# A four-layer graph network on one core: layer 1's order and buffers, and a dense first block in layer 2

## The chip, the core and the metric

The kernel runs on one core of one Trainium2 chip. The core has a matrix engine (PE, with its weight loads shown apart as PEld), a vector engine (DVE), a scalar engine (ACT), a general engine (POOL) that here mostly issues gathers, and a queue engine (SP) that issues plain transfers. Sixteen DMA engines move the data. The metric is the time of one execution in device microseconds; less is better. All data is float32.

## What is computed

There are 2708 nodes with 512 features each, and a 2708 x 2708 adjacency matrix in which about 0.15% of the entries and the diagonal are not zero (uniform between 0.05 and 1). Four layers follow each other, each with a residual sum and a layer norm:

```python
x = layernorm(x + L0(x, adj))
x = layernorm(x + L1(x, adj))
x = layernorm(x + L2(x, adj))
x = layernorm(x + L3(x, adj))

# L0:  (x - (adj @ x) * (diag + 1)) @ W + b
# L1:  h = x @ W_sa;  e = where(adj != 0, exp(-leaky_relu(s_left[:, None] + s_right[None, :])), 0)
#      x_a = (e / (e.sum(1) + 1e-5)) @ h;  x_b = adj @ (x @ W_gc) + b_gc
#      sigmoid(gate_a * x_a + gate_b * x_b)     # the gates from adj @ x and x
# L2:  head = (adj > 0); head = head / max(sqrt(sum(head * head, -1)), 1e-12)
#      inc = adj + head;  (inc @ x) / inc.sum(-1)
# L3:  A = adj + I; d = A.sum(0) ** -0.5;  tanh((d * A * d) @ x @ W.T + b)
```

In layer 2 the row norm of `head` depends on the row alone, so an entry of `inc` is the value of the edge plus one number of its row wherever the value is positive.

## The kernel before

Rows are cut into 24 blocks (`NB`) of 113 nodes (`R`); the last has 109. There are 22 windows (`KB`) of 128 nodes as well, for the dense projections of layer 0. Nothing is planned at run time: each engine executes its instructions in the order in which the code writes them, and waits where another engine's or a transfer's result is needed.

In layer 0 (to some 413 us of the span) the columns of the adjacency for a block are loaded (`load_adj`, L673 and L677), the edges are found on DVE, and each block gets a list of at most 512 source nodes (four chunks, `EC`), with values in `edges`. The rows of x are gathered, and each block writes a row of 1029 numbers (`W1`) per node into a table in DRAM, `table[0]`. All layers after that work from the lists: POOL gathers the 512 source rows of a block with four indirect transfers (`gather`, L600), and PE multiplies them by a 512 x 113 selection matrix that DVE builds from the list.

**Layer 1** (some 411 to 615 us). For each block, POOL gathers four times 128 x 1029 from `table[0]`, and for the blocks from 6 on also the block's own rows (`gather_own1`, L1382) into one of `NO` = 6 places in buffers that are no longer used; the first six own blocks come by plain loads at the end of layer 0 (`load_own1`). PE forms two sums: `sums1` (l1s, L1427) and `scored_sums1` (l1e, L1437). DVE works through `both1` (L1472 to L1483), `scores1` (L1410, L1414), `stats1` (L1492 to L1508, with a power on POOL in L1509), `gates1`, `gated1` (L1457, L1461, which read l1s), `mask1` (L1420), and `source_sum`. `norm1` (ACT, L1524) writes the normed rows into SBUF (`xr`) and SP stores them to `table[1]`. The l1s sum has one buffer in PSUM. At the end of layer 1 the column sums of the adjacency go through DRAM (`deg_d`, `deg_r`, L1556 and L1558), and the bias and weight of layer 3 (`b3`, `w3`) are loaded by SP.

**Layer 2** (some 615 to 768 us). Each block gathers four times 128 x 512 from `table[1]`. DVE rebuilds the selection matrix (`values`, L1294) and adds the norm of the row (`incidence`, L1612 and L1615; the norms come from `row_norms`, turned across by `turn_norm` on PE and copied by `copy_norm`). `aggregate` on PE makes l2a, `stats2` and `norm2` finish a block and store it to `table[2]`. `keep_warm` puts matmuls on PE that no one reads (`unread`, L1571). Layer 3 gathers from `table[2]`, sums, projects, and writes the output.

Every transfer of a block's 113 rows goes through `move_rows`, which issues two:

```python
c = r // 16 * 16
for a, b in ((0, c), (c, r)):
    if a < b:
        nc.sync.dma_start(out=dst(a, b), in_=src(a, b))
```

The end of layer 1 reads, in the order of the code: `both1(23)`, `stats1(23)`, `scale1`, `norm1(23)`, then `values(0)`, `incidence(0)`, `values(1)`, `incidence(1)`, then the gathers of layer 2's blocks 0 and 1, and the loop over 24 blocks.

Of the kernel before, what the change touches and what calls it, by code (L numbers as in the profile page):

```python
# [8 lines left out]
FP = mybir.dt.float32  # L9
AF = mybir.ActivationFunctionType  # L10
ALU = mybir.AluOpType
# [436 lines left out]
def sparse_stack(  # L448
# [115 lines left out]
    def move_rows(r, dst, src):  # L564

        c = r // 16 * 16
        for a, b in ((0, c), (c, r)):
            if a < b:
                nc.sync.dma_start(out=dst(a, b), in_=src(a, b))

    def turned(u, r, name):

        tr = ps_tr.tile([P, DB, P], FP, tag="tr", name=f"tr_{name}")
        for f in range(DB):
            nc.tensor.transpose(tr[:, f, :r], u[:r, f * P : (f + 1) * P], ident[:r, :r])
        uT = work.tile([P, DB, P], FP, tag="uT", name=f"uT_{name}")
        nc.scalar.copy(uT[:, :, :r], tr[:, :, :r])  # L577
        return uT

# [46 lines left out]

    w0_own = big.tile([P, 2 * W1], FP, name="w0_sb")
    w0_sb = w0_own[:, : DB * D].rearrange("p (b d) -> p b d", d=D)
    NO = 6

    def own_place(i):
        return (*shared, w0_own)[i % NO // 2][:, i % 2 * W1 :][:, :W1]

    def load_own1(i):
        r = rows(i)
# [12 lines left out]
    with ExitStack() as phase:  # L648
# [40 lines left out]

        def load_own(i):  # L690
            r = rows(i)
            xi = work.tile([P, D], FP, tag="xi", name=f"xi{i}")
            move_rows(r, lambda a, b: xi[a:b, :], lambda a, b: x[i * R + a : i * R + b, :])
            return xi

# [122 lines left out]
        def turn_w(k):  # L818
            ps = ps_tr.tile([P, DB, P], FP, tag="tr", name=f"w_sa_t{k}")
            for f in range(DB):  # L820
                nc.tensor.transpose(ps[:, f, :], w_sa_sb[:, f, k * P : (k + 1) * P], ident)
            wT = work.tile([P, DB, P], FP, tag="uT", name=f"w_saT{k}")
            nc.scalar.copy(wT, ps)
            w_saT[k] = wT

# [225 lines left out]
        def store0(w):  # L1051
            r = wrows(w)
            st, o = st0.pop(w)
            nc.scalar.copy(st[:r, D + 1 : 2 * D + 1], o[:r, :])
            move_rows(
                r, lambda a, b: table[0][w * P + a : w * P + b, :], lambda a, b: st[a:b, :]
            )
# [3 lines left out]
        def turn_u(i):  # L1061

            u, r = u0.pop(i), rows(i)
            tr = ps_tr.tile([P, DB, P], FP, tag="tr", name=f"tr_l0_{i}")
            for f in range(DB):
                nc.tensor.transpose(tr[:, f, :r], u[:r, f * P : (f + 1) * P], ident[:r, :r])
            a = i * R
            while a < i * R + r:
                w = a // P
                b = min(i * R + r, (w + 1) * P)  # L1070
                if w not in window_uT:
                    window_uT[w] = work.tile(
                        [P, DB, P], FP, tag="uw", name=f"uw{w}", bufs=3
                    )
                nc.scalar.copy(
                    window_uT[w][:, :, a - w * P : b - w * P], tr[:, :, a - i * R : b - i * R]
                )
                a = b
# [130 lines left out]
        for k in range(NB + 2):  # L1209
            m = k + 2  # L1210
            w, wx, rest = window_at.get(k), window_at.get(k - 1), window_at.get(k - 1)
            bare = 2 < k < NB and w is None
            after = 2 < k < NB and wx is None
            parts = 4
            if any(t not in window_at for t in (k + 1, k + 2, k + 3)) and 2 < k < NB - 4:
                parts = 5
            if bare:
                parts, rest = 2, None
            if after:
                parts, rest = 3, window_at[k - 2]  # L1220
            if wx is not None and k <= NB:
                turn_x(wx)
            if m < NB:
                ranges(m)
                mark(m)
                fetch(m)
            if w is not None:
                project0(w)
            if k == 1:
                times_a(2)  # L1230
                times_a(3)
            if k == 0:
                times_a(0)
                turn_w(2)
            if unstored:
                store0(unstored.pop())
            if k + 3 < NB:
                negatives(k + 3)
            search(1)
            if m < NB:  # L1240
                pick(m)
                own[m] = load_own(m)
                values0(m)
            if k == 1:
                score_rows()
            if w is not None:
                bias0(w)
            search(1)
            if w is not None:
                residual0(w)  # L1250
            if window_at.get(k + 1, 0) > 1:
                load_window(window_at[k + 1])
            search(parts - 2)
            if wx is not None and not bare:
                next0(wx)
            if w is not None:
                norm0(w)
            if k + 1 < NB:
                sums0(k + 1)
                inputs0(k + 1)  # L1260
            if k == 1:
                score_columns()
            if k + 2 == NB:
                worst = check_lists()
                for i in range(4):
                    load_own1(i)
            if k == 0:
                times_a(1)
                turn_w(3)
            if bare:  # L1270
                starts(m + 1)
                next0(wx)
            elif rest is not None:
                rest0(rest, lambda: turn_x(w) if k == NB else starts(m + 1) if m + 1 < NB else None)
                unstored.append(rest)
            elif m + 1 < NB:
                starts(m + 1)
            if k + 1 < NB:
                turn_u(k + 1)
            if k == NB:  # L1280
                tell(worst)
                for i in range(4, NO):
                    load_own1(i)
        keep_busy(4)
        store0(KB - 1)


    gpool = ctx.enter_context(tc.tile_pool(name="gpool", bufs=1))
# [65 lines left out]
    nc.vector.memset(root, -0.5)  # L1354
    edge_s, edge_e, sum_s, sum_e, vb1, gate1, v1, mv2, unscaled = ({} for _ in range(9))
    phase = ctx.enter_context(ExitStack())
    ps_1s = phase.enter_context(tc.tile_pool(name="ps_1s", bufs=1, space=bass.MemoryType.PSUM))
    ps_1e = phase.enter_context(tc.tile_pool(name="ps_1e", bufs=1, space=bass.MemoryType.PSUM))
    ps_sp = phase.enter_context(tc.tile_pool(name="ps_sp", bufs=2, space=bass.MemoryType.PSUM))

# [230 lines left out]
            nc.scalar.sqrt(inv_norm[:, at], inv_norm[:, at])  # L1591
            nc.vector.reciprocal(inv_norm[:, at], inv_norm[:, at])

    row_in, inc2 = {}, {}

    def turn_norm(i):

# [10 lines left out]
    def incidence(i, s):  # L1608
# [5 lines left out]
        )  # L1614
        nc.vector.tensor_add(inc, inc, s)  # L1615

    b3_bc = gpool.tile([P, D], FP, name="b3_bc")
    w3_sb = shared[0][:, : DB * D].rearrange("p (b d) -> p b d", d=D)

# [9 lines left out]
    for i in range(NB):  # L1629
# [5 lines left out]
        if i + 2 < NB:  # L1635
            values1(i + 2, (0, 1))
        scored_sums1(i)
        if i + 1 == NB:
            turn_norm(0)
            turn_norm(1)  # L1640
        if i + 1 < NB:
            scores1(i + 1)
        if 0 < i < NB - 1:
            stats1(i - 1)
        if 0 < i and i - 1 + NO < NB:
            gather_own1(i - 1 + NO)
        gates1(i)
        if i + 2 < NB:
            values1(i + 2, (2, 3))
# [12 lines left out]
            nc.sync.dma_start(out=w3_sb, in_=w3T.rearrange("(b p) o -> p b o", p=P))  # L1662
        if i < KB:
            source_sum(i)
        if i == KB:
            source_sums_out()
            row_norms(slice(0, KB))
    copy_norm(0)
    copy_norm(1)
    keep_warm(ps_sp, "sp", [P, 4, P], 8)  # L1670
    both1(NB - 1)
    spread_row(b3_bc, "b3")
    stats1(NB - 1)
    scale1()
    norm1(NB - 1)
    deg_ps = source_sums_in()
    inc_s = [values(0)]
    incidence(0, inc_s[0])
    inc_s.append(values(1))
    incidence(1, inc_s[1])  # L1680
    nc.vector.tensor_copy(b3_bc, spread_ps["b3"])

    nc.vector.tensor_copy(deg[:R, :], deg_ps[:R, 0, :NB])
# [5 lines left out]
    nc.vector.tensor_add(d_inv, deg, zero)  # L1689
    nc.scalar.sqrt(d_inv, d_inv)  # L1690
    row_norms(slice(KB, NB), False)
    phase.close()
    ps_agg = ctx.enter_context(tc.tile_pool(name="ps_agg2", bufs=2, space=bass.MemoryType.PSUM))
    ps_tr = ctx.enter_context(tc.tile_pool(name="ps_tr2", bufs=1, space=bass.MemoryType.PSUM))
    ps_o = ctx.enter_context(tc.tile_pool(name="ps_o2", bufs=2, space=bass.MemoryType.PSUM))
    ps_sp = ctx.enter_context(tc.tile_pool(name="ps_sp2", bufs=2, space=bass.MemoryType.PSUM))
    ps_u = ctx.enter_context(tc.tile_pool(name="ps_u", bufs=1, space=bass.MemoryType.PSUM))


    for i in range(2):  # L1700
        gather(gath[i], i, table[1], D)
    nc.vector.tensor_add(rowsum, rowsum, adiag)
    nc.vector.tensor_mul(plus, plus, inv_norm)
# [11 lines left out]
    dself = const.tile([P, NB], FP, name="dself")  # L1715
    nc.vector.scalar_tensor_tensor(dself, adiag, 1.0, d_inv, op0=ALU.add, op1=ALU.mult)

    sum2, v2, edge_3 = {}, {}, {}

    def own2(i):  # L1720
        r = rows(i)
        v = work.tile([P, D], FP, tag="v", name=f"l2v{i}")
        nc.scalar.activation(v[:r, :], xr[:r, i, :], AF.Copy, scale=plus[:r, i : i + 1])
        v2[i] = v

    def stats2(i):
# [32 lines left out]
        move_rows(r, lambda a, b: table[2][i * R + a : i * R + b, :], lambda a, b: y[a:b, :])  # L1759

    own2(0)
    for i in range(NB):
        if i + 2 < NB:
            gather(gath[(i + 2) % NGB], i + 2, table[1], D)
            turn_norm(i + 2)
# [1 line left out]
        sum2[i] = aggregate(inc2.pop(i), gath[i % NGB], rows(i), f"l2a{i}")  # L1767
        if i + 1 < NB:
            keep_warm(ps_u, "u", [P, D], 1)
        if i > 0:  # L1770
            stats2(i - 1)
        s = values((i + 2) % NB)
        if i > 0:
            norm2(i - 1)
        if i + 1 < NB:
            own2(i + 1)
        if i + 2 < NB:
# [133 lines left out]
```

## Time and profile before

| what | value |
| --- | --- |
| median of 14 runs | 978.04 us (972.11 to 983.77) |
| the profiled execution | 976.4 us, its span 974.7 us |
| granted TensorE clock, mean | 0.968 |
| busy share of the span | PE 91%, DVE 70%, ACT 54%, POOL 48% |
| first l1s matmul of block 1 and of block 23 | 429.9 and 604.8 us |
| first layer-2 gather on POOL | 623.73 us |
| indirect gathers by list: from the tables, from x | 288 and 96 |

The page of the profile has the busy time of each engine, a strip of the span in 40 slices, the DMA queues, the chain of waits that ended last, and the costliest groups of instructions. A group's row names the line of the code, the engine, the operation, what it writes and reads, how often, its busy time in us and the mean of one in ns, and the idle time of the engine just before it with what ended it. The waits view sums, by waiting instruction and releaser, how long an engine stood. The timeline lists single instructions with start and length in us. Besides these the trace has a record of every DMA packet, with its size and the time it took, and one of every rise of a DMA's semaphore.

### The profile page before, as it was taken

To read this page: it belongs to the slowest core of one execution; us is meant where nothing else is said; L and a number is where in the kernel's file an instruction comes from. 1 tells how busy PE (TensorE), PEld (TensorE's weight loads), DVE (VectorE), ACT (ScalarE), POOL (GpSimd) and SP (SyncE) were. 2 spreads that over 40 slices of the span, in tenths; PEclk is the share of its full clock that TensorE was granted. 3 is DMA by queue.
4 is the path that set the end of the run, shared out by engine and by line. 5 is a ranking of instruction groups with operands and counts; after the bars stand their busy time and mean duration, and the time that the engine had idled before them with its cause. 6 is when DMAs were issued, how large, how long until landed. Compare 5 with 4: busy or idle time off the path is not lost.

```text
span 974.7 us, 11098 instructions
## 1 busy us (share of the span) xinstructions
PE 883.5 (91%) x2957; PEld 488.9 (50%) x2957; DVE 686.7 (70%) x1811; ACT 527.2 (54%) x1221; POOL 471.1 (48%) x521
## 2 busy tenths in 40 slices
PE   6789999999999999989989899786979889999993
PEld 2445656555555555457767677332323333444441
DVE  7797899888998833268988888766768326555553
ACT  5686767767768743457777776343535212222221
POOL 3332323313233310167777673477777476676730
PEclk7799999999999999999999999897999999999997
DMA  9988786988886534388989994466767465555531
GB/s 246 313 206 226 212 228 202 262 221 227 221 234 202 168 110 144 106 302 301 331 315 326 324 319 162 131 196 190 208 203 213 119 174 157 152 167 170 151 106 33
DMA packets 133759, 201.74 MB, mean 207 GB/s; under 512 B 82700, under 2 KB 82746, under 8 KB 133689
## 3 DMA queue, kind: packets, MB, share of 16 engines
q0 software_dynamic: 39456, 120.08, 39.9%
q1 hardware_dynamic: 94233, 80.86, 29.1%
q8 instruction: 26, 0.43, 0.2%
q14 instruction: 44, 0.36, 0.1%
HBM read 183.00 MB, written 27.80 MB: 216 GB/s over the span
## 4 chain that ended last, share of the span: by engine, by line
PE 58%; DVE 12%; issue 11%; DMA 9%; POOL 4%; ACT 2%; SPq 2%; another core or an unknown queue 1%; DVEq 0%; POOLq 0%; ACTq 0%
PE o_l L584 14%; PE l3a L613 9%; PE l2a L613 7%; DMA gath<-table,source 6%; PE h L584 6%; PE l0a L613 6%; PE hb L584 5%; POOL gath L600 3%; PE unread L1571 3%; PE fetched L915 2%; SPq L677 1%; PE l1s L1427 1%; DMA gath<-in_x_dram 1%; DVE where_all L862 1%
## 5 line engine op out<-in xcount | busy, mean ns | idle before, releaser
L600 POOL DMA_INDIRECT gath<-table,source x288 | 309.5, 1075 | 108.0 <-issue 81.9
L600 POOL DMA_INDIRECT gath<-in_x_dram,source x96 | 97.5, 1016 | 222.4 <-issue 191.0
L1427 PE MATMUL l1s<-gath,s 128*113 128x256 f32 (+3 forms) x384 | 90.2, 387 | 19.4 <-DVE l1b L1457 14.4
L613 PE MATMUL l2a<-gath,s_left 128*113 128x512 f32 (+1 forms) x192 | 95.7, 631 | 8.8 <-DMA gath<-table,source 6.7
L613 PE MATMUL l3a<-gath,s 128*113 128x512 f32 (+1 forms) x192 | 89.9, 612 | 2.8 <-DMA gath<-table,source 2.8
L584 PE MATMUL o_l<-shared,uT_l 128*113 128x512 f32 (+1 forms) x192 | 86.5, 593 | 2.6 <-ACT uT_l L577 2.6
L1437 PE MATMUL l1e<-gath,e 128*113 128x257 f32 (+3 forms) x384 | 87.1, 379 | 0.9 <-issue 0.9
L1427 PEld LDWEIGHTS l1s<-gath,s 128*113 128x113 f32 (+1 forms) x384 | 65.9, 177 | 43.8 <-DVE l1b L1457 19.8
L613 PE MATMUL l0a<-gath,s 128*113 128x512 f32 (+1 forms) x192 | 87.7, 599 | 0.0
L584 PE MATMUL hb<-w_gc_sb,uT_x 128*128 128x512 f32 (+1 forms) x176 | 83.3, 601 | 0.0
L584 PE MATMUL h<-w_sa_sb,uT_x 128*128 128x259 f32 (+1 forms) x352 | 80.8, 382 | 0.0
L584 PE MATMUL o_l<-w_sb,uw 128*128 128x512 f32 (+1 forms) x176 | 80.3, 599 | 0.2
L1437 PEld LDWEIGHTS l1e<-gath,e 128*113 128x113 f32 (+1 forms) x384 | 68.0, 177 | 16.4 <-issue 1.3
L584 PEld LDWEIGHTS h<-w_sa_sb,uT_x 128*128 128x128 f32 (+1 forms) x352 | 64.8, 185 | 19.8 <-issue 6.1
L613 PEld LDWEIGHTS l2a<-gath,s_left 128*113 128x113 f32 (+1 forms) x192 | 32.3, 185 | 62.4 <-issue 33.2
L1830 ACT ACTIVATE y<-l3v,mv_l 113x512 f32<-113x512 f32 (+1 forms) x24 | 19.6, 816 | 80.7 <-DVE mv_l L1826 74.9
L584 PEld LDWEIGHTS o_l<-shared,uT_l 128*113 128x113 f32 (+1 forms) x192 | 33.9, 178 | 51.0 <-issue 47.3
L1804 DVE SCALAR_TENSOR_TENSOR l3v<-o_l,d_inv,b_bc 113x512 f32<-113x512 f32 (+1 forms) x25 | 18.1, 729 | 57.6 <-PE o_l L584 50.3
L1571 PE MATMUL unread<-bg_bc,ident 128*128 128x512 f32 x80 | 41.7, 636 | 16.6 <-remote 13.3
L613 PEld LDWEIGHTS l3a<-gath,s 128*113 128x113 f32 (+1 forms) x192 | 33.2, 184 | 42.3 <-issue 39.3
L613 PEld LDWEIGHTS l0a<-gath,s 128*113 128x113 f32 (+1 forms) x192 | 34.0, 180 | 40.3 <-issue 35.8
L1294 DVE TENSOR_SCALAR s<-niota_r,nrow,edges 128x113 f32<-128x113 f32 x192 | 51.9, 347 | 0.0
(250 smaller groups left out, 1591.7 us busy)
## 6 DMA issues: line engine op xcount, KB each, us to landing
shared<-in_adj_dram SPq DMA_DIRECT2D x14, 1186.5 KB
table<-st SPq DMA_DIRECT2D x21, 514.5 KB
gath<-in_adj_dram SPq DMA_DIRECT2D x7, 1186.5 KB
gath<-in_x_dram SPq DMA_DIRECT2D x21, 256.0 KB
xi<-in_x_dram SPq DMA_DIRECT2D x23, 224.0 KB
table<-xr SPq DMA_DIRECT2D x23, 224.0 KB
table<-y SPq DMA_DIRECT2D x23, 224.0 KB
out_dram<-y SPq DMA_DIRECT2D x23, 224.0 KB
```

Source lines behind the costliest of these rows:

```text
L584: nc.tensor.matmul(o, lhsT=uT[:, f, :r], rhs=w[:, f, :], start=(f == 0), stop=(f == DB - 1))
L600: nc.gpsimd.indirect_dma_start(out=g[:, c, :n], out_offset=None, in_=src[:, :], in_offset=bass.IndirectOffsetOnAxis(ap=source[:, i, c : c ...
L613: nc.tensor.matmul(agg[:r, :], lhsT=s[:, c, :r], rhs=g[:, c, off : off + D], start=(c == 0), stop=(c == EC - 1),)
L677: nc.sync.dma_start(out=a[:TAIL, NF, :r], in_=adjT[NF * P :, at])
L862: nc.vector.max_index(out=where_all[:, i, g * 8 : (g + 1) * 8], in_max=top, in_values=seg)
L915: nc.tensor.matmul(t["fetched"][:, c, : 3 * NS], lhsT=t["q"][:, c * P : (c + 1) * P], rhs=rec_all[:, i].rearrange("p k s -> p (k s)"), sta ...
L1294: nc.vector.tensor_scalar(s[:, c, :], niota_r, nrow[:, i, c : c + 1], edges[:, i, c, 1:2], op0=ALU.is_equal, op1=ALU.mult,)
L1427: nc.tensor.matmul(sum_s[i][:r, k, : at.stop - at.start], lhsT=s[:, c, :r], rhs=g[:, c, at], start=(c == 0), stop=(c == EC - 1),)
L1437: nc.tensor.matmul(sum_e[i][:r, k, k : k + at.stop - at.start], lhsT=e[:, c, :r], rhs=g[:, c, at], start=(c == 0), stop=(c == EC - 1),)
L1571: nc.tensor.matmul(o[:, :cols], lhsT=ident, rhs=bg_bc[:, :cols], start=True, stop=True)
L1804: nc.vector.scalar_tensor_tensor(v[:r, at], o[:r, at], d_inv[:r, i : i + 1], b3_bc[:r, at], op0=ALU.mult, op1=ALU.add,)
L1830: nc.scalar.activation(y[:r, :], v[:r, :], AF.Identity, bias=mv[:r, 3:4], scale=mv[:r, 2:3])
```

## The change

It has three parts.

1. The buffers `xi`, `uT` and `uw` of layer 0, which came from a pool, become slots of two larger tiles, `xi_own` and `uw_own`, with as many slots each as the pool gave them. The two tiles hold three more places for own rows in layer 1 (`NO` 9 in place of 6): `load_own1(6)` is issued with 4 and 5, 7 and 8 at the end of layer 0, and 15 own gathers are left in layer 1 of 18.
2. In layer 1, l1s gets two buffers in PSUM in place of one, and `gather_own1` moves ahead of `stats1`.
3. In layer 2, block 0 is not gathered. `load_all` loads the whole columns of block 0 of the adjacency, 2708 rows of 113 numbers, into the two tiles, at the end of the iteration `i == KB`; `incidence_all` adds the norm on DVE (two instructions for four node blocks), and `sums_all` multiplies them on PE with `xr` in SBUF, 24 matmuls. The parts are spread over the end of layer 1 as the diff shows; 8 warm-up matmuls leave there. The norms of block 0 are made earlier, and the gathers begin with blocks 1 and 2.

```diff
-    NO = 6
+    uw_own = big.tile([P, 3 * D], FP, name="uw_own")
+    xi_own = big.tile([P, max(4 * D, 2 * W1)], FP, name="xi_own")
...
+    NO = 9
...
             if k == NB:
                 tell(worst)
-                for i in range(4, NO):
+                for i in range(4, 7):
                     load_own1(i)
         keep_busy(4)
         store0(KB - 1)
+        for i in range(7, NO):
+            load_own1(i)
...
-    ps_1s = phase.enter_context(tc.tile_pool(name="ps_1s", bufs=1, space=bass.MemoryType.PSUM))
+    ps_1s = phase.enter_context(tc.tile_pool(name="ps_1s", bufs=2, space=bass.MemoryType.PSUM))
...
+    NX = xi_own.shape[1] // R
+    all_in = [
+        t[:, : n * R].rearrange("p (b i) -> p b i", i=R)
+        for t, n in ((xi_own, NX), (uw_own, NB - NX))
+    ]
+    def load_all():
+        for t, a, b in ((all_in[0], 0, NX), (all_in[1], NX, NB - 1)):
+            nc.sync.dma_start(
+                out=t[:R, : b - a, :],
+                in_=adjT[a * R : b * R, :R].rearrange("(b p) i -> p b i", p=R),
+            )
+        b = NB - 1
+        nc.sync.dma_start(out=all_in[1][: rows(b), b - NX, :], in_=adjT[b * R :, :R])
+    def incidence_all(blocks):
+        for b in blocks:
...
+            nc.vector.scalar_tensor_tensor(
+                inc[:R, :n, :], t[:R, at, :], 0.0,
+                row_in[0][:R, None, :].to_broadcast([R, n, R]), op0=ALU.is_gt, op1=ALU.mult,
+            )
+            nc.vector.tensor_add(t[:R, at, :], t[:R, at, :], inc[:R, :n, :])
+    def sums_all(blocks):
...
+        for b in blocks:
+            nc.tensor.matmul(
+                sum2[0][:R, :], lhsT=all_in[b >= NX][: rows(b), b - NX * (b >= NX), :],
+                rhs=xr[: rows(b), b, :], start=(b == 0), stop=(b + 1 == NB),
+            )
...
         if i + 1 < NB:
             scores1(i + 1)
+        if 0 < i and i - 1 + NO < NB:
+            gather_own1(i - 1 + NO)
         if 0 < i < NB - 1:
             stats1(i - 1)
-        if 0 < i and i - 1 + NO < NB:
-            gather_own1(i - 1 + NO)
...
+        if i == NB - 4:
+            row_norms(slice(0, 1))
         if i == KB:
             source_sums_out()
-            row_norms(slice(0, KB))
-    copy_norm(0)
+            row_norms(slice(1, KB))
+            load_all()
+        if i + 1 == NB:
+            incidence_all((0, EC))
     copy_norm(1)
-    keep_warm(ps_sp, "sp", [P, 4, P], 8)
+    copy_norm(2)
+    sums_all(range(2 * EC))
     both1(NB - 1)
-    spread_row(b3_bc, "b3")
     stats1(NB - 1)
+    incidence_all((2 * EC,))
     scale1()
     norm1(NB - 1)
+    sums_all(range(2 * EC, 3 * EC))
+    incidence_all((3 * EC,))
+    incidence_all((4 * EC, NX))
+    incidence_all(range(NX + EC, NB, EC))
+    sums_all(range(3 * EC, NX))
+    spread_row(b3_bc, "b3")
     deg_ps = source_sums_in()
-    inc_s = [values(0)]
-    incidence(0, inc_s[0])
-    inc_s.append(values(1))
-    incidence(1, inc_s[1])
+    sums_all(range(NX, NB))
+    inc_s = [values(1)]
+    incidence(1, inc_s[0])
+    inc_s.append(values(2))
+    incidence(2, inc_s[1])
...
-    for i in range(2):
+    for i in range(1, 3):
         gather(gath[i], i, table[1], D)
...
     own2(0)
-    for i in range(NB):
+    stats2(0)
+    own2(1)
+    phase.close()
...
+    for i in range(1, NB):
```

More of the change, by code (lines that the diff above doesn't have):

```diff
@@ L569, in move_rows, with next_uT @@
                 nc.sync.dma_start(out=dst(a, b), in_=src(a, b))
+    def next_uT():
+        uT_ring.append(uT_ring.pop(0))
+        return uT_ring[-1]
     def turned(u, r, name):
@@ L575, in turned @@
             nc.tensor.transpose(tr[:, f, :r], u[:r, f * P : (f + 1) * P], ident[:r, :r])
-        uT = work.tile([P, DB, P], FP, tag="uT", name=f"uT_{name}")
+        uT = next_uT()
         nc.scalar.copy(uT[:, :, :r], tr[:, :, :r])
@@ L628, in sparse_stack @@
     w0_sb = w0_own[:, : DB * D].rearrange("p (b d) -> p b d", d=D)
-    NO = 6
+    uw_own = big.tile([P, 3 * D], FP, name="uw_own")
+    uw_ring = [uw_own[:, k * D : (k + 1) * D].rearrange("p (b i) -> p b i", i=P) for k in range(3)]
+    xi_own = big.tile([P, max(4 * D, 2 * W1)], FP, name="xi_own")
+    xi_ring = [xi_own[:, k * D : (k + 1) * D] for k in range(2)]
+    uT_ring = [
+        xi_own[:, k * D : (k + 1) * D].rearrange("p (b i) -> p b i", i=P) for k in range(2, 4)
+    ]
+    NO = 9
     def own_place(i):
-        return (*shared, w0_own)[i % NO // 2][:, i % 2 * W1 :][:, :W1]
+        k = i % NO
+        t = (*shared, w0_own, uw_own, xi_own)[(k + (k >= 7)) // 2]
+        return t[:, (k + (k >= 7)) % 2 * W1 :][:, :W1]
     def load_own1(i):
@@ L691, in load_own @@
             r = rows(i)
-            xi = work.tile([P, D], FP, tag="xi", name=f"xi{i}")
+            xi = xi_ring[i % 2]
             move_rows(r, lambda a, b: xi[a:b, :], lambda a, b: x[i * R + a : i * R + b, :])
@@ L821, in turn_w @@
                 nc.tensor.transpose(ps[:, f, :], w_sa_sb[:, f, k * P : (k + 1) * P], ident)
-            wT = work.tile([P, DB, P], FP, tag="uT", name=f"w_saT{k}")
+            wT = next_uT()
             nc.scalar.copy(wT, ps)
@@ L1071, in turn_u @@
                 if w not in window_uT:
-                    window_uT[w] = work.tile(
-                        [P, DB, P], FP, tag="uw", name=f"uw{w}", bufs=3
-                    )
+                    window_uT[w] = uw_ring[w % 3]
                 nc.scalar.copy(
@@ L1592, in row_norms @@
             nc.vector.reciprocal(inv_norm[:, at], inv_norm[:, at])
-    row_in, inc2 = {}, {}
+    row_in, inc2, sum2 = {}, {}, {}
     def turn_norm(i):
@@ L1615, in incidence @@
         nc.vector.tensor_add(inc, inc, s)
+    NX = xi_own.shape[1] // R
+    all_in = [
+        t[:, : n * R].rearrange("p (b i) -> p b i", i=R)
+        for t, n in ((xi_own, NX), (uw_own, NB - NX))
+    ]
+    def load_all():
[8 more added lines that the diff above has]
+        for b in blocks:
+            t = all_in[b >= NX]
+            b = b - NX * (b >= NX)
+            at = slice(b, min(b + EC, t.shape[1]))
+            n = at.stop - at.start
+            inc = spool.tile([P, EC, R], FP, tag="e", name=f"all{b}")
+            nc.vector.scalar_tensor_tensor(
[4 more added lines that the diff above has]
+    def sums_all(blocks):
+        if 0 in blocks:
+            sum2[0] = ps_1s.tile([P, 2, D], FP, tag="s1", name="l2all")[:, 0, :]
+        for b in blocks:
[3 more added lines that the diff above has]
+            )
     b3_bc = gpool.tile([P, D], FP, name="b3_bc")
@@ L1637, in sparse_stack @@
         scored_sums1(i)
+        if i == NB - 3:
+            turn_norm(0)
+            copy_norm(0)
         if i + 1 == NB:
-            turn_norm(0)
             turn_norm(1)
+            turn_norm(2)
         if i + 1 < NB:
             scores1(i + 1)
+        if 0 < i and i - 1 + NO < NB:
+            gather_own1(i - 1 + NO)
         if 0 < i < NB - 1:
             stats1(i - 1)
-        if 0 < i and i - 1 + NO < NB:
-            gather_own1(i - 1 + NO)
         gates1(i)
@@ L1691, in sparse_stack @@
     row_norms(slice(KB, NB), False)
[L1692 to L1697, printed above, removed]
-    for i in range(2):
+    for i in range(1, 3):
         gather(gath[i], i, table[1], D)
@@ L1716, in sparse_stack @@
     nc.vector.scalar_tensor_tensor(dself, adiag, 1.0, d_inv, op0=ALU.add, op1=ALU.mult)
-    sum2, v2, edge_3 = {}, {}, {}
+    v2, edge_3 = {}, {}
     def own2(i):
@@ L1722, in own2 @@
         v = work.tile([P, D], FP, tag="v", name=f"l2v{i}")
-        nc.scalar.activation(v[:r, :], xr[:r, i, :], AF.Copy, scale=plus[:r, i : i + 1])
+        nc.scalar.activation(v[:r, :], xr[:r, i, :], AF.Copy, scale=plus[:r, i : i + 1] if i else 1.0)
         v2[i] = v
@@ L1761, in sparse_stack @@
     own2(0)
-    for i in range(NB):
+    stats2(0)
+    own2(1)
+    phase.close()
+    ps_agg = ctx.enter_context(tc.tile_pool(name="ps_agg2", bufs=2, space=bass.MemoryType.PSUM))
+    ps_tr = ctx.enter_context(tc.tile_pool(name="ps_tr2", bufs=1, space=bass.MemoryType.PSUM))
+    ps_o = ctx.enter_context(tc.tile_pool(name="ps_o2", bufs=2, space=bass.MemoryType.PSUM))
+    ps_sp = ctx.enter_context(tc.tile_pool(name="ps_sp2", bufs=2, space=bass.MemoryType.PSUM))
+    ps_u = ctx.enter_context(tc.tile_pool(name="ps_u", bufs=1, space=bass.MemoryType.PSUM))
+    for i in range(1, NB):
         if i + 2 < NB:
@@ L1769, in sparse_stack @@
             keep_warm(ps_u, "u", [P, D], 1)
-        if i > 0:
+        if i > 1:
             stats2(i - 1)
         s = values((i + 2) % NB)
-        if i > 0:
-            norm2(i - 1)
+        norm2(i - 1)
         if i + 1 < NB:
```

## The prediction

> **What bounds the kernel now.** I read the page's head first, then windows of the layers, then the waits of each engine in layer 1, then the timeline of the seam between layers 1 and 2, where most of the edit lands.
>
> ```profile
> PE 883.5 (91%) x2957; PEld 488.9 (50%) x2957; DVE 686.7 (70%) x1811; ACT 527.2 (54%) x1221; POOL 471.1 (48%) x521
> ```
>
> TensorE at 91% looks like the bound, but the average hides that each layer has another one. Two windows, with columns stretch, its length, the busy time of PE, PEld, DVE, ACT, POOL, then clock, DMA share and GB/s:
>
> ```profile
> 430.00:600.00 170.00, 153.97 (x685) 119.72 (x686) 149.63 (x387) 125.86 (x317) 117.61 (x111) 1.00 0.88 308
> 640.00:755.00 115.00, 96.02 (x220) 36.84 (x218) 79.62 (x217) 52.22 (x98) 87.44 (x80) 0.94 0.70 203
> ```
>
> In layer 1 (first row) PE and DVE are both near 90%; who waits for whom in that stretch decides (waits view, us in total, times, longest):
>
> ```profile
> DVE e L1410 <- DMA gath<-table,source: 4.6, 6, 1.0
> DVE l1b L1457 <- ACT row_cnt L1451: 3.8, 12, 0.3
> DVE l1b L1457 <- issue: 2.6, 8, 0.3
> DVE e L1410 <- issue: 1.7, 2, 1.0
> PE l1s L1427 <- DVE l1b L1457: 14.1, 12, 1.6
> ```
>
> PE waits for DVE; DVE never waits for PE, only for late gathers and for ScalarE's gate. So DVE is the bound of layer 1. From the timeline, the first l1s matmuls of blocks 1 and 23 stand at 429.9 and 604.8: 174.9 us over 22 blocks, 7.95 each, with DVE's own work at about 7.54.
>
> In layer 2 the groups view of 640 to 755 shows the issue of gathers on POOL, with hardly an idle moment longer than the 0.30 us between two:
>
> ```profile
> L600 POOL DMA_INDIRECT gath<-table,source x80 | 87.7, 1096 | 27.9 <-issue 18.6 <-PE l2a L613 3.8 <-remote 3.6
> L613 PE MATMUL l2a<-gath,s_left 128*113 128x512 f32 x161 | 78.4, 622 | 4.9 <-DMA gath<-table,source 3.4 <-issue 1.3
> ```
>
> 87.7 + 27.9 us for 20 blocks is 5.78 per block, while PE needs 78.4 / 20 = 3.9 and a warming matmul or two. Layer 2 is therefore a chain that begins with its first gather and runs at POOL's pace. The seam before it, from the timeline (start, length):
>
> ```profile
> 609.40 0.29 SPq L1558 DMA_DIRECT2D deg_r<-deg_d  x1
> 613.63 0.15 DVE L1472 SCALAR_TENSOR_TENSOR rec<-l1e,ediag 109x1 f32<-109x1 f32 x1
> 620.02 0.76 SPq L569 DMA_DIRECT2D table<-xr  x2
> 620.17 0.63 DVE L1612 SCALAR_TENSOR_TENSOR s_left<-s,row_in 128x452 f32<-128x452 f32 x1
> 620.83 0.63 DVE L1615 TENSOR_TENSOR s_left<-s_left,s 128x452 f32<-128x452 f32 x1
> 623.73 1.08 POOL L600 DMA_INDIRECT gath<-table,source  x1 [4.78 <-PE unread L1571]
> ```
>
> The last block's both1 starts on DVE at 613.63, its normed rows are stored at 620.02, and layer 2's first gather goes at 623.73. The page names a PE warm-up as releaser, but POOL's sequencer passed the store's semaphores at 622.88 to 622.97, and the remaining marks within 0.8 us: the store's landing, then POOL's handling of it. Whatever delays that store delays all that follows, one for one.
>
> **Layer 1, small gains.** The ring buffers have the counts that the pool gave and no new waits. With l1s in two PSUM slots PE's 14.1 us of waiting for l1b goes, but PE is not late: by itself worth nothing, for DVE comes next. The own gather ahead of stats1 lets POOL issue it before its power (0.71 us, itself waiting for DVE); the gathers behind were what DVE waited for (4.6 + 1.7 us in 170). Over 22 blocks that is 6.3 x 175 / 170 = 6.5; three own gathers less (1.07 + 0.30 each) help POOL only. The ceiling is the 22 x (7.95 - 7.54) = 9. I take 5 and keep 2 to 8. The two places more cost two stores' worth of loads ahead of layer 1's first gathers, in a stretch where DMA idles: 0 to 2.6, I take 1.2. Net -3.8.
>
> **Layer 2, one block less.** Block 0's four gathers and its two DVE groups leave; POOL's chain starts with block 1 and has 23 blocks: 5.7 us less. Its price on PE, 24 matmuls with 512 columns, is 20.6 us: each is two records on PE, and those of the warm-ups in the seam start 0.43 us apart at full clock (0.86 a matmul). Eight warm-ups leave; PE has that time in what follows, and stats2(0) only has to be done before PE's second block.
>
> **The load of the dense block.** load_all puts three DMAs on SP right behind deg_r, that is at about 609.75: 113x18x113, 113x5x113 and 109x113 numbers, 2034 + 565 + 109 = 2708 rows of 452 bytes (the last 436). Layer 0 has loads of the same bytes, 128 partitions at a time: its 452-byte packets take 29.3 ns in the mean and 26 in the median on 16 engines, so 2708 packets / 16 x 29.3 = 5.0 us. If load_all spreads like that, it costs about that. But the trace also shows on how many engines a load of SP's runs: after issue its semaphore rises once at once and then once for each engine that has finished. A 128-row load has 16 rises; the 20-row one of L677 has 1 + 10; deg_d with 22 rows 1 + 11; deg_r with 24 rows 1 + 12; those of 2 to 15 rows have one landing for each row, and a 1-row one has 1 + 1. In every case that is the largest divisor of the row count that is no more than 16. 113 and 109 have no divisor but 1 below 17. And every other move of a block in this kernel is cut into 112 + 1 rows. So I price load_all at one engine, with 16 engines as the other end; no row shows a 113-row load itself.
>
> The Trainium skill, "DMA: Bandwidth & Descriptors", section on why a DMA increments its semaphore by 16, says that a DMA takes the largest count up to 16 that divides the slowest dimension of both sides, and names 127 partitions as running on one engine. The landings above agree at 1, 10, 11, 12 and 16; by that rule alone load_all is on one engine for sure, by the nearest load of this size (128 rows) on 16.
>
> On one engine at 26 ns (the median, as nothing else loads beside it): 52.9 + 14.7 + 2.8 = 70.4 us; at the mean 29.3: 59.6 + 16.6 + 3.2 = 79.4. The first packet comes about 1.4 us after issue (as for the load issued at 52.4), at 611.2, so the first part is there at 664 and all at 682.
>
> Who waits: (1) DVE. incidence_all of the first eight groups stands ahead of both1(23) and needs the first part: both1(23) moves from 613.6 to 665 + 2 x 1.25 = 667.5, and its store's issue, 6.4 later in the timeline above and 0.5 more for the third group (the rest of its 1.25 fits into DVE's 0.76 us of waiting for POOL's power), to 674.4. All of block 23's end, stats1 and norm1, is queued behind that wait. (2) SP. norm1(21)'s and norm1(22)'s stores, b3 and w3 come behind load_all on the same queue, and norm1(23)'s two stores reuse the semaphores of load_all's second and third part, so that the last store can't be issued before 682.5; on that one engine its rows stand behind 32 packets of w3, some 3 us. (3) POOL: it has nothing but gathers of table1, which wait for those stores. Landing at about 687, first gather at about 688 in place of 623.7: +64. DVE's later groups and PE's dense matmuls are done by then or in the 5 us until the first gathered rows land, at half clock too (the clock drops to 0.5 for 3 to 10 us after idle stretches at 628.9 and 663).
>
> **Sum.** +64.3 - 5.7 - 3.8 = +54.8 on the profiled execution's 976.4: 1031; the median of the runs shown is 1.6 above that: 1033. Ends: 29.3 ns, 1 to 2 us more in the queue, least gain in layer 1: +73 - 5.7 + 0.6 = +68, 1046. Fastest packets (16 engines at their peak start one per 22.5 ns each), stores not held behind the load and only DVE's wait paid, most gain: both1(23) at 662, gather at 672, +48 - 5.7 - 8 = +35, 1013.
>
> **Rivals.** *The load spreads over 16 engines* (0.06). For it: all large loads in this trace do. Then the first part lands at 614.8, both1(23) follows two groups later at 617.4, which is +3.8, and the third group adds 0.5: gather +4.3; one block less -5.7; layer 1 -3.8; PE catching up on 20.6 us of dense matmuls +0.7: -4.5, so 971.9 for the profiled execution and 973.5 for the median. Not slower. The price falls with the number of engines: with 7 the first part (52.9 / 7) lands at 619.1 and both1(23) starts 8.0 late, with the 0.5 just what the other terms bring (5.7 + 3.8 - 0.7); with 6 or fewer the load decides. *Only DVE pays* (0.2, inside the forecast's side): the last store is not held behind the load, and all that counts is the first part: issue at 674.4, gather 3.7 later at 678, which is 1023, and 1013 with the fastest packets. *Layer 1 gives nothing* because DVE's floor is already met: the same +64 - 5.7 + 1.2, 1038; it moves the result by 4 and no sign.
>
> **Chances.** The forecast with its variants 0.93, the spreading load 0.06, the rest 0.01. About 0.3% (3 us) is what a measurement here tells from no change; the spreading case at 973.5, with 969 to 979 by its terms' bounds, is faster by more than that three times in four. Faster 0.04, same 0.02, slower 0.94. The range takes the slow side's ends, 1013 to 1046, and holds 8 in 10.
>
> **What would show it.** In the profile after: SP's load of xi_own at about 606 to 610 with a semaphore that rises 1 + 1; DVE idle for some 50 us ahead of its first e<-xi_own group, released by that DMA; DMA share near 0.06 of 16 engines over 70 us; PE idle or at half clock; the first table1 gather near 685 and 23 blocks behind it at 5.7 to 5.8. In layer 1, no wait of l1s for l1b, and 7.7 per block instead of 7.95. Wrong: 16 landings, a DVE wait below 5 us, and a total under 980.

## The result: 1027.2 us after 977.7

The changed kernel takes 1027.23 us (median of 10 runs, 1024.56 to 1031.04); the kernel before, with more runs added, 977.69 (47 runs). The ratio is 1.0504, 95% interval 1.0480 to 1.0529: 5% slower, and 6 us under the predicted 1033. The profiled execution took 1029.6 us with a span of 1027.8, 53.2 more than the one before.

The timeline of SP in the changed kernel shows the load (lines of it, start and length in us):

```profile
602.76 0.29 SPq L1572 DMA_DIRECT2D deg_r<-deg_d  x1
603.23 0.24 SPq L1641 DMA_DIRECT2D xi_own<-in_adj_dram  x1
603.57 47.35 SPq L1641 DMA_DIRECT2D uw_own<-in_adj_dram  x1
650.97 13.35 SPq L1646 DMA_DIRECT2D uw_own<-in_adj_dram  x1
664.41 3.65 SPq L569 DMA_DIRECT2D table<-xr  x4
668.51 0.40 SPq L1718 DMA_DIRECT2D shared<-in_L_gnn_W_dram  x1
669.01 1.66 SPq L569 DMA_DIRECT2D table<-xr  x2
```

The first part is issued in 0.24 us. The second, which only has to be handed over as well, holds SP for 47 us and the third for 13: with 2034 rows on the way SP could not even issue the next load, and norm1(21)'s store waits behind it until 664; w3 and the last block's stores go out at 668.5 and 669 to 670.7. The semaphore of each of the three loads rises once at once and once more when the load has landed (1 + 1): one engine each. The first part lands 50.9 us after its issue, the last at 670.3.

DVE's waits from 600 to 690 (us in total, times, longest), and POOL's first gather of layer 2:

```profile
DVE all L1655 <- DMA xi_own<-in_adj_dram: 47.1, 1, 47.1
DVE all L1655 <- DMA uw_own<-in_adj_dram: 4.7, 2, 3.4
```

```profile
676.92 1.08 POOL L604 DMA_INDIRECT gath<-table,source  x1 [14.83 <-DMA table<-xr]
```

DVE's 47.1 us stand ahead of both1(23); the 4.7 for the other two parts come after block 23's norm. The first gather stood at 623.73. Its releaser is the last store, as predicted. What the core does meanwhile is a window of 43 us (busy time of PE, PEld, DVE, ACT, POOL, clock, DMA share, GB/s):

```profile
612.00:655.00 43.00, 0.00 (x0) 0.00 (x0) 0.82 (x2) 0.00 (x0) 0.00 (x0) 0.50 0.07 19
```

Every compute engine stands (DVE has two instructions, 0.82 us), the granted clock is 0.50, and the DMA share of 0.07 is about one engine of sixteen.

Layer 1 did get faster. From the first l1s matmul to the end of the last l1e it took 418.1 to 612.0 before, 193.9 us, and takes 418.2 to 605.0, 186.8. A block takes 7.71 us in place of 7.95 (first l1s matmuls of blocks 1 and 23 at 427.3 and 597.0). The waits of 430 to 600:

```profile
DVE l1b L1471 <- ACT row_cnt L1465: 5.1, 13, 1.2
DVE l1b L1471 <- issue: 2.2, 7, 0.3
PE l1e L1451 <- DVE l1a L1492: 8.4, 13, 1.1
```

DVE's 6.3 us of waiting for gathers are gone, its waits at l1b, for ScalarE's gate, are about as before (7.3 in place of 6.4), and PE waits for DVE still, now at l1e in place of l1s.

### The profile page after: what moved, and what is told of

Its sections match the earlier page's. It is cut to its first block, busy times and chain, and to the rows that moved or that the text cites. A ratio compares the mean times of both kernels' runs of the same rounds, so it can differ in the third digit from the quotient of the medians.

```text
span 1027.8 us, 11210 instructions
## 1 busy us (share of the span) xinstructions
PE 896.2 (87%) x2979; PEld 495.0 (48%) x2979; DVE 689.7 (67%) x1822; ACT 525.6 (51%) x1221; POOL 459.0 (45%) x515
## 3 DMA queue, kind: packets, MB, share of 16 engines
q1 hardware_dynamic: 97334, 83.48, 28.5%
## 4 chain that ended last, share of the span: by engine, by line
PE 62%; DVE 14%; another core or an unknown queue 7%; ACT 5%; DMA 4%; issue 4%; SPq 2%; POOL 1%; DVEq 0%; POOLq 0%; ACTq 0%
PE o_l L588 14%; PE l3a L617 8%; PE l2a L617 8%; PE hb L588 7%; PE h L588 7%; PE l0a L617 6%; PE l2all L1665 2%; PE unread L1585 2%; PE fetched L929 2%; DMA gath<-table,source 1%; DVE l1b L1471 1%; SPq L691 1%; DVE l1b L1475 1%; DMA gath<-in_x_dram 1%
## 5 line engine op out<-in xcount | busy, mean ns | idle before, releaser
L604 POOL DMA_INDIRECT gath<-table,source x284 | 297.3, 1047 | 126.3 <-issue 65.6
L588 PE MATMUL o_l<-shared,xi_own 128*113 128x512 f32 (+1 forms) x192 | 88.6, 605 | 5.9 <-issue 5.2
L588 PE MATMUL hb<-w_gc_sb,xi_own 128*128 128x512 f32 (+1 forms) x176 | 83.3, 601 | 0.0
L588 PE MATMUL h<-w_sa_sb,xi_own 128*128 128x259 f32 (+1 forms) x352 | 80.8, 382 | 0.0
L588 PE MATMUL o_l<-w_sb,uw_own 128*128 128x512 f32 (+1 forms) x176 | 79.9, 597 | 0.2
L588 PEld LDWEIGHTS h<-w_sa_sb,xi_own 128*128 128x128 f32 (+1 forms) x352 | 64.8, 185 | 19.8 <-issue 6.1
L1665 PE MATMUL l2all<-xr,xi_own 113*113 113x512 f32 x36 | 18.6, 682 | 50.3 <-DVE xi_own L1659 50.3
L588 PEld LDWEIGHTS o_l<-shared,xi_own 128*113 128x113 f32 (+1 forms) x192 | 34.7, 182 | 55.6 <-issue 54.7
L1501 ACT ACTIVATE l1v<-l1v 113x512 f32<-113x512 f32 (+1 forms) x24 | 15.2, 632 | 83.7 <-DVE l1v L1497 69.2
L1585 PE MATMUL unread<-bg_bc,ident 128*128 128x512 f32 x62 | 34.6, 664 | 21.7 <-remote 21.6
```

The source lines that it names most:

```text
L588: nc.tensor.matmul(o, lhsT=uT[:, f, :r], rhs=w[:, f, :], start=(f == 0), stop=(f == DB - 1))
L604: nc.gpsimd.indirect_dma_start(out=g[:, c, :n], out_offset=None, in_=src[:, :], in_offset=bass.IndirectOffsetOnAxis(ap=source[:, i, c : c ...
L1501: nc.scalar.activation(v[:r, :], v[:r, :], AF.Tanh, scale=0.5)
L1585: nc.tensor.matmul(o[:, :cols], lhsT=ident, rhs=bg_bc[:, :cols], start=True, stop=True)
L1665: nc.tensor.matmul(sum2[0][:R, :], lhsT=all_in[b >= NX][: rows(b), b - NX * (b >= NX), :], rhs=xr[: rows(b), b, :], start=(b == 0), stop=( ...
```

## The experiments

Medians of the kernel before differ by some us between the chips that ran the groups (977.7, 981.5, 982.1, 981.6), so ratios to before on the same chip are compared; 0.1% is 1 us. The times in the expectations were reckoned from the 977.7, so a time of the later groups reads some 4 us high against them.

**How many engines.** Three kernels change nothing but the cut of load_all's rows; the last block's 109 rows are cut into 96 + 13, 106 + 3 and 102 + 7.

```diff
-                out=t[:R, : b - a, :], in_=adjT[a * R : b * R, :R].rearrange(...)
+            for p, q in ((0, 112), (112, 113)):      # e1;  (0, 106), (106, 113): e2;  (0, 102), (102, 113): e3
+                nc.sync.dma_start(out=t[p:q, : b - a, :], in_=src[p:q])
...
```

e1, 112 + 1 rows:

> Only load_all is changed: each of its three loads is cut into two, 112 + 1 rows of every node block and 96 + 13 of the last, as every other transfer of this kernel is. Theory (one engine): the 112-row loads show 16 landings in place of one, the first part lands some 5 us after its issue at about 603 in place of 51, DVE's wait for it falls from 47.1 us to 0 to 3, the first gather of layer 2 goes at 619 to 623 in place of 676.9, and the time falls by 54 to 58 us from the 1027.2 of the changed kernel, to 969 to 974. Rival (the many small packets cost, or the place of the dense block's work ahead of both1(23), whatever the engines): the wait stays over 30 us and the time over 1005.

e2, 106 + 7 rows:

> load_all's loads are cut into 106 + 7 rows (106 + 3 for the last block); 106 is 2 x 53. Theory (the largest divisor up to 16 sets the engines): the 106-row loads show two landings; 1908 packets on two engines at the 24.4 ns of the changed kernel are 23.3 us, so DVE waits 20 to 23 us in place of 47.1, and the time is 990 to 996. Rival (any cut lets it spread over all engines): a wait of 0 to 3 us and 969 to 974. Rival (the cut changes nothing): 1027.

e3, 102 + 11 rows:

> load_all's loads are cut into 102 + 11 rows (102 + 7 for the last block); 102 is 6 x 17. Theory: six landings; 1836 packets on six engines at 24.4 ns are 7.5 us, DVE waits 4 to 7 us, and the time is 974 to 979, close to before: the point at which the prediction's sum changes sign was 7 engines. Rival (spread over all or over none): 969 to 974, or 1027.

| load_all | rises of the large part's semaphore | its landing after issue | DVE's wait | ratio to before (95%) |
| --- | --- | --- | --- | --- |
| uncut, 113 rows | 1 + 1 | 50.9 us | 47.1 us | 1.0504 (1.0480 to 1.0529) |
| e2, 106 + 7 | 1 + 2 | 25.1 | 21.9 | 1.0172 (1.0111 to 1.0232) |
| e3, 102 + 11 | 1 + 6 | 10.7 | 7.7 | 0.9992 (0.9964 to 1.0020) |
| e1, 112 + 1 | 16 | 5.7 | 2.1 | 0.9979 (0.9949 to 1.0008) |

DVE's waits in e2, e3 and e1, one row of each:

```profile
DVE all L1657 <- DMA xi_own<-in_adj_dram: 21.9, 1, 21.9
```

```profile
DVE all L1657 <- DMA xi_own<-in_adj_dram: 7.7, 1, 7.7
```

```profile
DVE all L1657 <- DMA xi_own<-in_adj_dram: 2.1, 1, 2.1
```

Same bytes, same rows, same place in the program: the wait goes with the number of engines. The rivals (small packets as such, or the place of the work, whatever the engines; any cut spreads) are out. e3's wait of 7.7 us is over its 4 to 7. Six engines give no change, which agrees with the break-even of 7 in the prediction; the intervals for six and for sixteen overlap, so these runs do not place it closer. e1's time was expected at 969 to 974 and came at 977.2 beside 981.5 of before, 4.3 less by medians and 0.2% by the ratio, whose interval reaches from -0.5% to +0.1%. The cut wins back all of the 5%, but block 0's dense sum then brings nothing that can be seen: e6 below, the same change without the dense sum, has 975.2 on the same chip (0.9953 to before). The seam says why:

```profile
623.58 1.08 POOL L604 DMA_INDIRECT gath<-table,source  x1 [4.65 <-issue]
```

From the end of l1e at 606.8 to this gather are 16.8 us, 11.7 before: 2.1 of waiting, 2.5 for two DVE groups ahead of both1(23), 0.5 of the third. That is 5.1 paid, for a block that saved 4.2 in the mean of the profiles (below).

**The load issued earlier.** e5 has the cut of e1 and e4 has none; both issue load_all three iterations earlier.

```diff
+        if i == NB - 5:
+            load_all()
...
             row_norms(slice(1, KB))
-            load_all()
```

> The 112 + 1 cut, and load_all is issued three iterations earlier, at the end of i == 19, in the midst of layer 1's gathers. Theory: the load is done before DVE comes to it, so DVE waits nothing; against the cut alone it gains the 1 to 2 us that are left of the wait and loses what 4 us of all DMA engines cost layer 1's gathers (DMA share 0.85 there), 0 to 3: 967 to 974. Rival (layer 1 is so close to the DMA engines' limit that the load costs its full length there): 973 to 978.

> load_all uncut, on one engine, but issued three iterations earlier, at about 566 in place of 603. Theory: the load is still on one engine, which it now shares with layer 1's gathers; if the two alternate by packet, few of its packets pass before the last gathers land at about 590, and DVE waits 15 to 35 us: 985 to 1015. If the load has the engine to itself its first part lands at 617 and DVE waits some 10 us (985 to 990), but layer 1's gathers wait for that one engine. Rival (the wait is not for the load's landing): 1027.

e5 has no wait left and its gather goes 14.6 us after l1e's end:

```profile
623.10 1.08 POOL L604 DMA_INDIRECT gath<-table,source  x1 [4.64 <-issue]
```

The ratio is 0.9930 (0.9897 to 0.9963), 974.7 us beside 981.5. It is the lowest here, under both kernels, though its interval overlaps with those of e1, and of e6 and e8 below. The rival, that layer 1 pays the load's full length, is not borne out: from layer 1's first gather to the end of the last l1e it takes 195.7 us, and 196.2 in e1. e4's DVE waits 28.5 us, within its 15 to 35, but the time is 1018.8 (one run), 4 over the range:

```profile
581.65 55.20 SPq L1641 DMA_DIRECT2D uw_own<-in_adj_dram  x1
636.90 13.58 SPq L1646 DMA_DIRECT2D uw_own<-in_adj_dram  x1
650.58 4.36 SPq L569 DMA_DIRECT2D table<-xr  x6
```

SP came to the load at 581.6 and not 566, since a store ahead of it in the queue had to wait; then it was held 69 us, and the stores of six blocks, the degree's way through DRAM and w3 went out after 650. The first part took 58.5 us in place of 50.9 beside the gathers. Starting early saves only part of the loss, 36.7 us over before on that chip in this one run in place of 49.5, while the load holds the queue of all the stores behind it.

**DVE or the stores.** e9 leaves the loads uncut and moves the second and third part behind norm1(23)'s stores.

```diff
-            load_all()
+            load_all(0)          # the first part
...
     norm1(NB - 1)
+    load_all(1)                  # the other two
```

> The changed kernel with its uncut loads, but the second and third part (565 and 109 rows of 452 bytes) are issued after norm1(23)'s stores in place of ahead of norm1(21)'s. It separates the two that wait for the load: DVE for the first part, and SP with the last store for the other two. Theory (both wait, one after the other): DVE's wait for the first part stays at 46 to 48 us, but the first gather of layer 2 goes at 665 to 669 in place of 676.9, since the store no longer stands behind the load. The time hardly follows, because the dense sums then get their last part at about 683 and end at 687 or later, and PE is late for the second block: 1021 to 1030. Rival (only DVE's wait counts, the stores were never held): first gather at 676 to 678, and 1027. Rival (the first gather alone sets the time): 1016 to 1019.

The first part's load, the stores of two blocks behind it (four transfers in one line) and layer 2's first gather:

```profile
609.06 0.24 SPq L1641 DMA_DIRECT2D xi_own<-in_adj_dram  x1
611.77 46.17 SPq L569 DMA_DIRECT2D table<-xr  x4
672.47 1.08 POOL L604 DMA_INDIRECT gath<-table,source  x1 [4.41 <-DMA table<-xr]
```

The first gather went at 672.47, 63.4 us after the first load's issue in place of 73.7: the store had been held for 10 us more by the other parts and by w3, as expected (the load was issued 5.8 us later than in the changed kernel, so the 665 to 669 expected become 671 to 675). The first part alone holds SP as well: norm1(21)'s store behind it, cut for 16 engines, took 45 us to issue. But the time was 1045.4 (1.0655, 1.0597 to 1.0712), not 1021 to 1030:

```profile
693.60 0.63 DVE L1657 SCALAR_TENSOR_TENSOR all<-uw_own,row_in 113x452 f32<-113x452 f32 x1 [23.27 <-DMA uw_own<-in_adj_dram]
694.94 7.88 PE L1667 MATMUL l2all<-xr,uw_own 113*113 113x512 f32 x12 [14.55 <-DVE uw_own L1661]
706.96 5.28 PE L617 MATMUL l2a<-gath,s_left 128*113 128x512 f32 x8 [4.04 <-DVE l2v L1792]
```

The second part, 565 rows, took 23.5 us beside layer 2's gathers where it takes 13.6 behind the first; DVE's work for blocks 1 and 2 and the degrees, some 8 us, is queued behind that wait; and PE came to block 1 at 707. Both rivals are out: the gather moved with the store, and it did not set the time. POOL then stood 22.9 us for a free gather buffer. An early first gather is worth nothing if the dense sum is this late. In the changed kernel the two meet: the dense sum is done at 680.5,

```profile
675.13 5.41 PE L1665 MATMUL l2all<-xr,uw_own 113*113 113x512 f32 x12
```

and the first block's rows can be put at 680.4, since PE began 3.5 us after the first gather before (623.7 to 627.2). Put in the same way, the dense sum ends 26.9 us behind the first rows in e9, but 10.4 in e1 and 9.1 in e5, and there layer 2 is not longer for it: 148.4 and 145.1 us from its first gather to that of layer 3, 148.4 before and 167.6 in e9. So some 10 us of lateness of the dense sum cost nothing that shows, and 27 cost about 20.

**Layer 1, its parts.** e6 is parts 1 and 2 of the change without the dense block; e7 and e8 make one edit each to the kernel before.

```diff
-    ps_1s = phase.enter_context(tc.tile_pool(name="ps_1s", bufs=1, ...))      # e7
+    ps_1s = phase.enter_context(tc.tile_pool(name="ps_1s", bufs=2, ...))
...
+        if 0 < i and i - 1 + NO < NB:                                           # e8: ahead of
+            gather_own1(i - 1 + NO)                                             # stats1
         if 0 < i < NB - 1:
             stats1(i - 1)
```

> The first two parts alone: ring buffers, nine places for own rows, two l1s buffers, own gather ahead of stats1; layer 2 as before the change, with block 0 gathered. By the trace of the changed kernel, whose last l1e sum ends at 605.0 in place of 612.0, the time is 7 us under before: 969 to 972. By the prediction's own terms (5 less for the loop, 1.2 more for the loads): 3.8 under, 973 to 975. Rival (layer 1 gains nothing, the shift of 7 is of layer 0): 977 to 979.

> The kernel before with one edit: l1s in two PSUM buffers. By the prediction (DVE is the bound of layer 1, PE's wait for l1b is no loss): 0 to 1 us less, 976.5 to 978. Rival (a PE that runs ahead frees gather buffers earlier, so gathers come earlier): 2 to 6 us less, 971.5 to 975.5.

> The kernel before with one edit: the own gather ahead of stats1. By the prediction (DVE waits for gathers that POOL issues late, behind its power and the own gather): 3 to 6 us less, 971.5 to 974.5, and no wait of DVE for gathers left in layer 1. Rival (POOL is as late as before, since its gathers wait for PE to free the buffer): within 1 us of before.

| kernel | first l1s to last l1e | per block, 1 to 23 | ratio to before (95%) |
| --- | --- | --- | --- |
| before | 193.9 us | 7.95 us | 1 |
| e7, two l1s buffers | 193.0 | 7.98 | 0.9996 (0.9971 to 1.0021) |
| e8, own gather first | 186.7 | 7.72 | 0.9955 (0.9932 to 0.9978) |
| e6, both and nine places | 185.4 | 7.66 | 0.9953 (0.9921 to 0.9986) |

The second column also has the start of the layer in it: the first l1s matmul comes 6.7 us after the first gather before and 9.2 and 9.3 in e8 and e6, so a stretch counted from there looks shorter by 2.5 us. The per-block figures, over 22 blocks 5.2 us for e8 and 6.4 for e6, are nearer to the times. In e7 DVE still waits for gathers, and PE has only moved its wait from l1s to l1e; in e8, with one l1s buffer, PE still waits for l1b (8.2 us in place of 14.1) and DVE hardly for gathers:

```profile
DVE e L1410 <- DMA gath<-table,source: 5.6, 6, 2.1
PE l1e L1437 <- DVE l1a L1478: 12.8, 13, 2.2
```

```profile
DVE e L1410 <- DMA gath<-table,source: 0.5, 1, 0.5
PE l1s L1427 <- DVE l1b L1457: 8.2, 15, 1.0
```

The gain of layer 1 is, within these intervals, the place of one gather. Taking away the wait that was longest (PE's 14.1 us at l1s) was worth nothing by itself; taking away most of the one of 6.3 us gave what e6 gives.

## Why the prediction was right, point by point

**One engine.** Right, and shown by e1 to e3: the number of landings of the other loads' semaphores was the clue. "DMA: Bandwidth & Descriptors" of the Trainium skill says, in the section on why a DMA increments its semaphore by 16, that a DMA takes the largest count up to 16 that divides the slowest dimension of both sides. The trace agrees, at 1, 2, 6 and 16 engines here.

**Its price per packet.** Predicted 26 ns, measured 24.3: the 2034 packets of the first part start from 604.12, 0.9 us after its issue (1.4 predicted), to 653.51, and the landing follows 0.6 later. All 2708 rows are of 452 bytes; the 436 of the prediction is a slip. Issue to last landing was 67.1 us for some 72 predicted. This is the main reason why the seam, from l1e's end to the first gather, was 60.2 us longer (71.9 after 11.7) and not 64.3. 26 was the median with 16 engines at work; alone an engine was somewhat quicker.

**Who waits.** DVE 47.1 us (some 50 expected), then the last store behind the rest of the load and w3. Both steps are shown by e9, and in the changed kernel the last store's second transfer goes out at 670.36, 0.02 us after the landing of the third part, whose semaphore it reuses as the prediction said. The variant that only DVE pays was wrong in mechanism. Whether it would be cheaper by the 10 us it names, no run shows: e9 frees the stores, but brings the last part later as well. Two figures of the working do not follow from its own terms: DVE's step takes 665 for a first part that is there at 664, and the low end has both1(23) at 662 where 611.2 + 45.8 + 2.5 us are 659.5, which would put that end at 1011 and not 1013. The sum of the forecast does not rest on either.

**Layer 1.** The 5 us for the loop hold: 7.71 us per block in place of 7.95 (7.7 predicted) are 5.3 over 22 blocks, and e6 is 0.47% faster, 4.6 us of 978. The 1.2 us more at the start, for the loads, do not show: the first gather of layer 1 went at 410.4 us (411.4 before). This does not settle their price, since it went at 411.6 in e8 without those loads and at 412.7 in e6 with them. That two PSUM buffers by themselves are worth nothing, and the own gather nearly everything, was right.

**One block less in layer 2.** 5.7 us were predicted. In the two profiles shown it is 0.4: from the first gather of layer 2 to that of layer 3, 148.4 us before and 148.1 after. One pair can't tell, since PE stops several times in this layer in every kernel; a stop near its end, like this one, has few blocks left in which to be made up:

```profile
797.67 3.60 PE L617 MATMUL l2a<-gath,s_left 128*113 128x512 f32 x8
807.28 2.07 PE L1585 MATMUL unread<-bg_bc,ident 128*128 128x512 f32 x2 [6.02 <-remote]
```

Over four profiles with 24 gathered blocks (before, e6, e7, e8: 148.4, 152.7, 151.6, 149.8) the mean is 150.6, over six with 23 (the changed kernel, e1 to e5: 148.1, 148.4, 146.4, 145.0, 145.5, 145.1; e9, held up by its dense sum, is left out) 146.4. That is 4.2 less: the term was right in kind. Either group spreads over some 4 us, so its size is not settled, and 5.7 is not excluded.

**The sum** of the profiled execution: -7.1 in layer 1, +60.2 in the seam, -0.4 in layer 2, +0.5 elsewhere, together +53.2, where -3.8, +64.3 and -5.7, together +54.8, were predicted. The total comes this near by luck in part: the seam and layer 1 came out 4.1 and 3.3 us lower than their terms and layer 2 5.3 higher, and these errors cancel. The medians are 49.5 apart, 4 us less than the profiled executions; a layer 2 of the mean length above would account for that, but no run shows that it does.

**The rival that the load spreads** was run as e1. Its mechanism holds: gather 5.1 late, for 4.3 priced. Its sum, -4.5 us or -0.46%, is inside the measured interval, near its lower end.

## What to carry to other kernels

Look at the first dimension of every transfer that is added beside a helper which cuts its rows: 113 is prime, and the cut into 112 + 1 that all other transfers of this kernel make was the difference between 51 and 6 us. Price a transfer not only by what waits for its bytes, but by the stores that are queued behind it on the same engine. And of several waits in a loop, look first at that of the engine that sets the pace: here its 6.3 us were worth removing, and the longest wait, PE's, was free.

## What the hardware showed that was not expected

A load that takes long holds the engine that issues the next one. SP needed 47.35 us to issue the second load and 13.35 for the third, against 0.24 to 0.40 for the loads around them. Cut for two engines, the second piece's issue took SP 21.3 us, for six 6.7 and for sixteen 1.4; the lines have both pieces of the first part together, in e2, e3 and e1:

```profile
608.55 21.59 SPq L1643 DMA_DIRECT2D xi_own<-in_adj_dram  x2
```

```profile
608.44 7.05 SPq L1643 DMA_DIRECT2D xi_own<-in_adj_dram  x2
```

```profile
605.02 1.77 SPq L1643 DMA_DIRECT2D xi_own<-in_adj_dram  x2
```

It is not peculiar to few engines: in layer 0 of the kernel before, the issue at 33.80 us took SP 7.65 behind a load on 16 engines that landed at 42.6 to 44.8.

The 24 ns per 452-byte packet hold for an engine by itself. Beside gathers of 2 KB rows one engine needed 23.5 us for 565 rows (e9, from the issue), 13.6 without them (the changed kernel, from the landing of the part before).

In e1 the one-row rest over 18 node blocks landed on 9 engines and that over 5 on 5: with one row, the next dimension is divided. The same section says so too, as it goes by the slowest dimension that is not of size 1.

PE's stops in layer 2 ("remote", 2 to 5 in each profile, up to 8 us; in the changed kernel's from 801.3 to 807.3 POOL goes on issuing gathers meanwhile) stay open. They are in every kernel, and no experiment was made on them.
